# A two-layer graph attention kernel on Trainium2: edge sums by quarters of the nodes, as float32 products

## The chip, the cores and the metric

The kernel runs on one core of a Trainium2 chip. The metric is device time in microseconds (us), the median of the runs. Before the change it is 2547.23 us (three runs, 2546.41 to 2550.64). One more execution was taken with the hardware profiler; it took 2188.15 us.

## The reference

There are 3125 nodes with 768 features and 53,125 edges, which come sorted by destination; each edge has one of three types. Both layers compute the same thing, layer 1 with four heads of 192 features, layer 2 with one head of 768:

```python
xr = jnp.einsum('nd,rdf->rnf', x, W)          # a row for each node and type
oi = xr[etype, dst]; oj = xr[etype, src]
alpha = leaky_relu(oi @ q + oj @ k, 0.2)
e = exp(alpha - segment_max(alpha, dst)[dst])
a = e / (segment_sum(e, dst)[dst] + EPS)
out = segment_sum(a[:, :, None] * oj, dst) + b
```

Between the layers stands an ELU. The output is `layernorm(x + out)`. All of it is float32.

## The kernel before

The nodes are cut into 25 groups of at most 128, so that the edges of a group fill at most 17 *slots* of 128 edges each (14 for the first group); there are 422 slots in all. As edges are sorted, a group's slots hold rising node numbers. In the drawn graph a group has 104 to 128 nodes and up to 2175 edges.

The program has three stages, and every engine's order is written out by hand: each stage is a loop over steps k, one slot a step, and a table of events says at which step each function puts its instructions on the engines' queues. An engine runs its queue in that order. Pools of buffers with a fixed number of copies (`bufs`) do the rest: a buffer is filled again only when its last reader is done.

- Stage one (`phase1`, to about 690 us) multiplies x by layer 1's weights (L698), puts the rows into a table in DRAM, and computes layer 1's attention weights p for every edge and head (`pall`). `a_last` (L586) sets a flag; when it isn't zero, a second, slower kernel for any input runs afterwards (L1295 on).
- Stage two (`phase2`, about 700 to 1548 us) sums layer 1's rows and multiplies the result by layer 2's weights. `gather` (L840) has POOL fetch the 128 rows of a slot (128 x 772 float32) by an indirect DMA into one of nine buffers. `high` (L848) has ACT scale each head's 193 columns (192 features and a one) by p and round them to float32r, in H, and has DVE or POOL make the selection matrix `sel`: row is the edge, column the node, one where the edge ends at that node. `low` (L866) has DVE compute what H left out, in L. `sums` (L879) then adds sel x H and sel x L into PSUM (`acc`), two products of 386 columns each. Both parts are float32r, which goes through TensorE once. The first four odd slots are instead taken "whole" (L844): DVE puts p into the selection, and the gathered rows are multiplied in float32. `e_y` to `e_s2` turn a finished group into ELU outputs and transpose them; `d_part` (L939) multiplies them by layer 2's weights, in 18 pieces of six products, one for nearly every slot; `d_row` (L952) has ACT copy the products, and SP's queue store them to the second table.
- Stage three (`phase3`, from about 1551 us) gathers layer 2's rows into 36 buffers, computes the attention weights of a group from one column of these rows (`a_spread` to `a_put`), and sums. Here 17 of each 25 slots are whole (L1126): ACT makes the selection with p by two activations (L1141, L1142), and TensorE multiplies it by the rows in float32. The others are split in two parts as in layer 1. `e_y` to `e_out` add x and the bias, normalise and store.

The lines that matter most for TensorE in the two sums are these:

```python
T.matmul(acc[:, c, :HW], sel, a[:, c * HW:(c + 1) * HW], ...)            # L894, for H and for L
T.matmul(acc[:, h // 2, c], sel[:, h], gs[k % NG][:, h * CW:(h + 1) * CW], ...)   # L888, whole
T.matmul(acc[:, c, :HW], sel, a[:, c * HW:(c + 1) * HW], ...)            # L1168, both kinds
```

Of the kernel before, what the change touches and what calls it, by code (L numbers as in the profile page):

```python
# [8 lines left out]
F32 = mybir.dt.float32  # L9
# [11 lines left out]
P = 128  # L21
# [16 lines left out]
SL = 17  # L38
# [7 lines left out]
WHOLE = (17, 25)  # L46
# [3 lines left out]
def kernel(  # L50
# [402 lines left out]
    ends = {base(b) + slots(b) - 1 for b in range(NB)}  # L453
# [65 lines left out]
    def phase1(pre, work, psum, wH, wL, qq):  # L519
# [66 lines left out]
        def a_last():  # L586

            V.tensor_scalar(oidx, n_all[:, NB - 1:NB], col, None, op0=ALU.add)
            V.tensor_scalar(starts[0:1, 2, :NB], n_all[0:1, :NB], float(N - P), None, op0=ALU.min)
            more = work.tile([1, 2], F32, name="more", bufs=1)  # L590
            V.tensor_single_scalar(more[:, 0:1], n_all[0:1, NB:NB + 1], float(N), op=ALU.is_lt)
            V.tensor_single_scalar(more[:, 1:2], n_all[0:1, NB - 2:NB - 1], float(N - P), op=ALU.is_gt)
            V.tensor_add(bad, bad, more)
            V.tensor_add(flag, bad[:, 0:1], bad[:, 1:2])
# [230 lines left out]
    def phase2(work, psum, wH, wL):  # L825
# [3 lines left out]
        gs = share  # L829
# [8 lines left out]
        ends2 = ends  # L838

        def gather(k):  # L840
            b, j = slot(k)
            gather_rows(gs[k % NG], tab1, b, j)

        def whole(k):  # L844

            return k < 8 and k % 2 == 1

        def high(k):  # L848
            b, j = slot(k)
            g = gs[k % NG]  # L850
            if whole(k):
                sel = work.tile([P, H1, P], F32, name="L", bufs=3)
                for h in range(H1):
                    V.tensor_scalar(sel[:, h], row, dl[:, b, j:j + 1], pall[:, b, j, h:h + 1],
                                    op0=ALU.is_equal, op1=ALU.mult)
                st[k] = sel
                return
            H = work.tile([P, RW], F32R, name="H", bufs=4)
            for h in range(H1):
                c = slice(h * CW, (h + 1) * CW)  # L860
                S.activation(H[:, c], g[:, c], AF.Copy, scale=pall[:, b, j, h:h + 1])  # L861
            sel = work.tile([P, P], F32R, name="sel", bufs=4)
            (V if k % 3 == 0 else G).tensor_scalar(sel, row, dl[:, b, j:j + 1], None, op0=ALU.is_equal)  # L863
            st[k] = [sel, H]

        def low(k):  # L866
            if whole(k):
                return
            b, j = slot(k)
            g = gs[k % NG]  # L870
            H = st[k][1]
            L = work.tile([P, RW], F32R, name="L", bufs=3)
            for h in range(H1):
                c = slice(h * CW, (h + 1) * CW)
                V.scalar_tensor_tensor(L[:, c], g[:, c], pall[:, b, j, h:h + 1], H[:, c].bitcast(F32),  # L875
                                       op0=ALU.mult, op1=ALU.subtract)
            st[k].append(L)

        def sums(k):  # L879
            b, j = slot(k)  # L880
            if j == 0:
                blk[b] = {"acc": psum.tile([P, 2, 512], F32, name="acc", bufs=2)}
            acc = blk[b]["acc"]
            if whole(k):
                sel = st.pop(k)
                for h in range(H1):
                    c = slice(h % 2 * CW, (h % 2 + 1) * CW)
                    T.matmul(acc[:, h // 2, c], sel[:, h], gs[k % NG][:, h * CW:(h + 1) * CW], start=False,  # L888
                             stop=(k in ends2), skip_group_check=True)
                return  # L890
            sel, H, L = st.pop(k)
            for i, a in enumerate((H, L)):
                for c in range(2):
                    T.matmul(acc[:, c, :HW], sel, a[:, c * HW:(c + 1) * HW], start=(j == 0 and i == 0),  # L894
                             stop=(k in ends2 and i == 1), skip_group_check=True)
# [77 lines left out]
        LAG = 8  # L973
# [16 lines left out]
        for k in range(max(ev) + 1):  # L990
# [9 lines left out]
            if 0 <= k - LAG + 2 < NK:  # L1000
                low(k - LAG + 2)
            if 0 <= k - LAG + 3 < NK:
                high(k - LAG + 3)
# [11 lines left out]
    def phase3(work, psum):  # L1015
# [3 lines left out]
        NG = 36  # L1019
# [106 lines left out]
        def whole(k):  # L1126

            return k % 3 == 0 if late(k) else k * WHOLE[0] % WHOLE[1] < WHOLE[0]

        def late(k):  # L1130

            return k >= NK - SL

        def high(k):
            b, j = slot(k)
            g = gs[:, k % NG, :]
            p = blk[b]["p"][:, j:j + 1]
            if whole(k):
                sel = work.tile([P, P], F32, name="selp", bufs=4)

                S.activation(sel, row, AF.Abs, bias=dl[:, b, j:j + 1], scale=-1.0)  # L1141
                S.activation(sel, sel, AF.Relu, bias=p, scale=blk[b]["np"][:, j:j + 1])  # L1142
                st[k] = [sel, g]
                return
            H = work.tile([P, RW], F32R, name="H", bufs=4)
            S.activation(H, g, AF.Copy, scale=p)  # L1146
            sel = work.tile([P, P], F32R, name="sel", bufs=4)
            (G if late(k) else V).tensor_scalar(sel, row, dl[:, b, j:j + 1], None, op0=ALU.is_equal)
            st[k] = [sel, H]

        def low(k):
            if whole(k):
                return
            b, j = slot(k)
            g = gs[:, k % NG, :]
            L = work.tile([P, RW], F32R, name="L", bufs=3)
            V.scalar_tensor_tensor(L, g, blk[b]["p"][:, j:j + 1], st[k][1].bitcast(F32), op0=ALU.mult, op1=ALU.subtract)  # L1157
            st[k].append(L)

        def sums(k):  # L1160
            b, j = slot(k)
            sel, *parts = st.pop(k)
            if j == 0:
                blk[b]["acc"] = psum.tile([P, 2, 512], F32, name="acc", bufs=2)
            acc = blk[b]["acc"]
            for i, a in enumerate(parts):
                for c in range(2):
                    T.matmul(acc[:, c, :HW], sel, a[:, c * HW:(c + 1) * HW], start=(j == 0 and i == 0),  # L1168
                             stop=(k in ends and i == len(parts) - 1))
# [54 lines left out]
        LAG = SL + 11  # L1224
        for b in range(NB):
# [7 lines left out]
            for d, f in ((2, a_alpha), (3, a_turn), (4, a_scan), (5, a_exp), (6, a_back), (7, a_put)):  # L1233
                when(e + d, f, b)
            if b + len(xbs) < NB:
                when(e + LAG + 20, x_load3, b + len(xbs))
            for d, f in ((1, e_y), (2, e_n), (5, e_sd), (6, e_low), (8, e_out)):
                when(e + LAG + d, f, b)
        for k in range(max(ev) + 1):
            if k < NK:  # L1240
                gather(k)
            if 0 <= k - LAG < NK:
                sums(k - LAG)
            for f, a in ev.get(k, []):
                f(*a)
            if 0 <= k - LAG + 2 < NK:
                low(k - LAG + 2)
            if 0 <= k - LAG + 3 < NK:
                high(k - LAG + 3)
# [580 lines left out]
```

## Time and profile before

| | before |
|---|---|
| median of the runs | 2547.23 us |
| profiled execution, its own time | 2188.15 us |
| its span, first to last instruction | 2186.4 us |
| busy: PE, PEld, DVE, ACT, POOL | 2015.1, 1730.7, 1458.8, 1356.5, 1674.3 us |
| granted TensorE clock, mean | 0.969 |
| moved by DMA | 506.04 MB, 231 GB/s |

PE is TensorE's products, PEld its weight loads, which run beside them; DVE is VectorE, ACT ScalarE, POOL GpSimd. A record of a product lasts from its start to its modelled end, and the next one starts before that end, so distances between starts are what a stream costs. In the timeline's rows the columns are the start, the length of the merged piece, the engine, the line, the operation, what it writes and reads, the shapes and the number of records; in brackets stands idle time before the piece and what ended it. A row of waits says who waited for whom, the total, the number of times and the longest.

### The profile page before, as it was taken

How to read it: one execution, taken by the hardware profiler on the slowest of the kernel's cores; microseconds unless marked ns; L12 is line 12 of the kernel's file. 1: busy time of each engine (PE TensorE's matmuls, PEld its weight loads, DVE VectorE, ACT ScalarE, POOL GpSimd, SP SyncE). 2: the span in 40 equal slices, each digit the busy share in tenths (PEclk: the TensorE clock that was granted, in tenths of full speed). 3: DMA queues.
4: the chain of work that ended last, by engine and by line, in shares of the span. 5: the costliest groups of instructions: out<-in, count | busy, mean ns of one | idle time of the engine just before them, and what ended most of it. 6: DMA issues, size and time to landing. Idle time of an engine off the chain costs nothing.

```text
span 2186.4 us, 37632 instructions
## 1 busy us (share of the span) xinstructions
PE 2015.1 (92%) x10953; PEld 1730.7 (79%) x10953; DVE 1458.8 (67%) x4031; ACT 1356.5 (62%) x3159; POOL 1674.3 (77%) x1615
## 2 busy tenths in 40 slices
PE   5979999999987799999999999999499999989997
PEld 5979998899887799999999999999355555555555
DVE  6535554454534899999999999998155555556555
ACT  5412111122111788888888888887268887878786
POOL 4257777777777888888888888886477777777774
PEclk9989999999998899999999999999799999999999
DMA  6555545545457977888787878786789998988883
GB/s 177 188 137 173 192 145 169 174 158 183 160 168 224 311 233 246 240 246 241 237 249 226 249 231 248 231 243 191 256 303 305 315 322 309 302 295 281 294 300 108
DMA packets 156842, 506.04 MB, mean 231 GB/s; under 512 B 43875, under 2 KB 57069, under 8 KB 156628
## 3 DMA queue, kind: packets, MB, share of 16 engines
q0 software_dynamic: 81904, 331.52, 49.9%
q1 hardware_dynamic: 64494, 156.04, 20.6%
q10 hardware_dynamic: 10230, 15.98, 2.2%
q8 instruction: 91, 1.49, 0.3%
q14 instruction: 123, 1.01, 0.2%
HBM read 412.55 MB, written 95.69 MB: 232 GB/s over the span
## 4 chain that ended last, share of the span: by engine, by line
PE 61%; POOL 12%; DMA 11%; issue 11%; DVE 3%; ACT 1%; POOLq 0%; SPq 0%; DVEq 0%; ACTq 0%
PE po L949 19%; PE acc L1168 14%; PE acc L894 12%; PE po L698 8%; POOL kt L461 8%; DMA G<-ftab,ridx 6%; POOL G L461 2%; DMA kt<-kt,ridx 1%; POOL share L461 1%; PE bank L282 1%; DVE L L875 1%; PE pt L260 1%; POOL sel L863 1%; PE pt L924 1%; PE po L396 1%
## 5 line engine op out<-in xcount | busy, mean ns | idle before, releaser
L861 ACT ACTIVATE H<-share,pall 128x193 fp32r<-128x193 f32 x1672 | 618.2, 447 | 104.7 <-PE acc L894 53.5
L875 DVE SCALAR_TENSOR_TENSOR L<-share,pall,H 128x193 fp32r<-128x193 f32 x1672 | 619.0, 435 | 28.2 <-issue 19.8
L949 PE MATMUL po<-wH,hT 128*128 128x386 f32 (+1 forms) x1800 | 529.1, 339 | 0.0
L461 POOL DMA_INDIRECT G<-ftab,ridx x374 | 416.0, 1112 | 113.9 <-issue 56.1
L461 POOL DMA_INDIRECT share<-ftab,ridx x374 | 437.0, 1168 | 80.4 <-DVE L L875 34.7
L461 POOL DMA_INDIRECT kt<-kt,ridx x374 | 396.3, 1060 | 114.0 <-issue 108.5
L698 PE MATMUL po<-wH,xT 128*128 128x384 f32 x1584 | 440.3, 348 | 8.8 <-ACT share L713 4.4
L1168 PE MATMUL acc<-G,selp 128*128 128x386 f32 x1124 | 417.1, 505 | 0.0
L949 PEld LDWEIGHTS po<-wH,hT 128*128 128x128 f32 x1800 | 334.1, 189 | 0.6 <-DVE hT L937 0.5
L698 PEld LDWEIGHTS po<-wH,xT 128*128 128x128 f32 x1584 | 294.6, 191 | 13.8 <-ACT share L713 6.2
L949 PE MATMUL po<-wL,hT 128*128 128x386 f32 (+1 forms) x900 | 304.8, 339 | 0.0
L1168 PEld LDWEIGHTS acc<-G,selp 128*128 128x128 f32 x1124 | 206.0, 193 | 118.7 <-issue 16.3
L698 PE MATMUL po<-wL,xT 128*128 128x384 f32 x792 | 270.3, 341 | 0.0
L894 PE MATMUL acc<-H,sel 128*128 128x386 f32 x836 | 227.0, 353 | 19.2 <-POOL sel L863 17.6
L713 ACT COPY share<-po 128x384 f32<-128x384 f32 x144 | 67.9, 478 | 275.0 <-PE po L698 268.9
L863 POOL TENSOR_SCALAR sel<-frow,fdl 128x128 fp32r<-128x128 f32 x278 | 219.0, 788 | 12.4 <-PE acc L894 1.7
L894 PE MATMUL acc<-L,sel 128*128 128x386 f32 x836 | 217.8, 342 | 0.0
L1157 DVE SCALAR_TENSOR_TENSOR L<-G,p,H 128x772 fp32r<-128x772 f32 x141 | 143.1, 1017 | 56.1 <-ACT H L1146 56.0
L894 PEld LDWEIGHTS acc<-H,sel 128*128 128x128 f32 x836 | 148.0, 190 | 36.0 <-POOL sel L863 33.7
L949 PEld LDWEIGHTS po<-wL,hT 128*128 128x128 f32 x900 | 169.6, 188 | 0.0
L894 PEld LDWEIGHTS acc<-L,sel 128*128 128x128 f32 x836 | 155.1, 191 | 0.2 <-DVE L L875 0.2
L698 PEld LDWEIGHTS po<-wL,xT 128*128 128x128 f32 x792 | 151.8, 192 | 0.0
(246 smaller groups left out, 2688.1 us busy)
## 6 DMA issues: line engine op xcount, KB each, us to landing
ftab<-share SPq DMA_DIRECT2D x75, 386.0 KB
ftab<-r SPq DMA_DIRECT2D x75, 386.0 KB
share<-in_L_gnn_W_dram SPq DMA_DIRECT2D x36, 384.0 KB
w_d<-w2hl SPq DMA_DIRECT2D x18, 768.0 KB
sT<-dr_d SPq DMA_DIRECT2D x25, 544.0 KB
share<-in_x_dram SPq DMA_DIRECT2D x25, 384.0 KB
xb_d<-share SPq DMA_DIRECT2D x25, 384.0 KB
xr<-in_x_dram SPq DMA_DIRECT2D x23, 384.0 KB
```

The costliest lines, as they stand in the source:

```text
L260: T.transpose(pt[:, f, c * P:(c + 1) * P], a[:, (2 * i + f) * P:(2 * i + f + 1) * P], ident)
L282: T.matmul(to, a[:, 2 * i + f, :], t[:, f, :w], start=(n == 0), stop=(n == 2 * DT - 1))
L461: return G.indirect_dma_start(out=to, out_offset=None, in_=tab, in_offset=_index(i[:, j:j + 1]), bounds_check=NP * R - 1, oob_is_err=False)
L698: m = T.matmul(po[:, :HALF], xT[:, s, t, :], w[:, i, sl], start=(n == 0), stop=(n == 3 * DT - 1))
L713: S.copy(to, po[:, :HALF].rearrange("p (h f) -> p h f", h=2))
L861: S.activation(H[:, c], g[:, c], AF.Copy, scale=pall[:, b, j, h:h + 1])
L863: (V if k % 3 == 0 else G).tensor_scalar(sel, row, dl[:, b, j:j + 1], None, op0=ALU.is_equal)
L875: V.scalar_tensor_tensor(L[:, c], g[:, c], pall[:, b, j, h:h + 1], H[:, c].bitcast(F32), op0=ALU.mult, op1=ALU.subtract)
L894: T.matmul(acc[:, c, :HW], sel, a[:, c * HW:(c + 1) * HW], start=(j == 0 and i == 0), stop=(k in ends2 and i == 1), skip_group_check=True)
L949: T.matmul(po[:, :wd], hT[:, k, t, :], w[:, r * DT + t, sl], start=(t == 0 and n == 0), stop=(t == DT - 1 and n == 2))
L1157: V.scalar_tensor_tensor(L, g, blk[b]["p"][:, j:j + 1], st[k][1].bitcast(F32), op0=ALU.mult, op1=ALU.subtract)
L1168: T.matmul(acc[:, c, :HW], sel, a[:, c * HW:(c + 1) * HW], start=(j == 0 and i == 0), stop=(k in ends and i == len(parts) - 1))
```

## The change

The 128 nodes of a group are cut into four quarters of 32. A slot's edges end in one or two neighbouring quarters, listed in `WINDOW` for each of the 17 slots. Both layers' sums become float32 products of the gathered rows with a selection of 32 columns that holds p, one product for each quarter of the slot, written to that quarter's 32 partitions of PSUM (and so on that quarter of TensorE's columns). The slots of a group are taken in seven rounds (`ROUNDS`) of two or three, whose quarters mostly differ, and a round's products are put on the queue together, one quarter after the other.

In stage two, `high` is four DVE operations on at most 64 columns, `low` and the copies to H go away, the rows are gathered in the rounds' order (`in_turn`), there are 14 row buffers for nine, and sums follow a gather by 6 steps, not 8. In stage three, `high` is two ACT operations on at most 64 columns (DVE's one for odd slots of the last group), all rounds of a group follow two steps apart once its weights p are there, and there are 44 row buffers for 36. A new test, at the start of stage three, counts the edges that lie outside their slot's quarters and adds the count to the flag, which is therefore set there and not in `a_last`.

```diff
+WINDOW = ((0,), (0,), (0,), (0, 1), (0, 1), (0, 1), (1,), (1, 2), (1, 2), (1, 2), (2,), (2, 3), (2, 3), (2, 3),
+          (2, 3), (3,), (3,))
+
+ROUNDS = ((0, 7, 15), (1, 8, 16), (2, 9), (3, 11), (4, 12), (6, 14, 10), (5, 13))
...
+    def rounds(b):
+        return [[j for j in r if j < slots(b)] for r in ROUNDS]
...
-        gs = share
+        gs = share + [work.tile([P, RW], F32, name=f"g{i}", bufs=1) for i in range(5)]
...
+        def in_turn(k):
+
+            b, i = slot(k)
+            return b, [j for r in rounds(b) for j in r][i]
 
         def gather(k):
-            b, j = slot(k)
-            gather_rows(gs[k % NG], tab1, b, j)
...
+            gather_rows(gs[k % NG], tab1, *in_turn(k))
 
         def high(k):
...
+            b, j = in_turn(k)
+            lo, hi = WINDOW[j][0] * 32, WINDOW[j][-1] * 32 + 32
+            sel = work.tile([P, H1, 64], F32, name="selp", bufs=6)
+            for h in range(H1):
+                V.tensor_scalar(sel[:, h, :hi - lo], row[:, lo:hi], dl[:, b, j:j + 1], pall[:, b, j, h:h + 1],
+                                op0=ALU.is_equal, op1=ALU.mult)
+            st[b, j] = sel, gs[k % NG]
...
+            o = [(i, t) for r in rounds(b) for i in r for t in WINDOW[i]]
+            for h in range(H1):
+                c = slice(h % 2 * CW, (h % 2 + 1) * CW)
+                for i, t in o:
+                    if i not in rounds(b)[n[0]]:
+                        continue
+                    u = [x for x, y in o if y == t]
+                    sel, g = st[b, i]
+                    T.matmul(acc[32 * t:32 * t + 32, h // 2, c], sel[:, h, 32 * (t - WINDOW[i][0]):][:, :32],
+                             g[:, h * CW:(h + 1) * CW], start=(i == u[0] and h % 2 == 0), stop=(i == u[-1]),
+                             skip_group_check=True)
...
-        LAG = 8
+        LAG = 6
...
-        NG = 36
+        NG = 44
...
+        def high(b, n):
+
+            for j in rounds(b)[n]:
+                p = blk[b]["p"][:, j:j + 1]
+                lo, hi = WINDOW[j][0] * 32, WINDOW[j][-1] * 32 + 32
+                sel = work.tile([P, 64], F32, name="selp", bufs=10)[:, :hi - lo]
+                if b == NB - 1 and j % 2:
+                    V.tensor_scalar(sel, row[:, lo:hi], dl[:, b, j:j + 1], p, op0=ALU.is_equal, op1=ALU.mult)
+                else:
+
+                    S.activation(sel, row[:, lo:hi], AF.Abs, bias=dl[:, b, j:j + 1], scale=-1.0)
+                    S.activation(sel, sel, AF.Relu, bias=p, scale=blk[b]["np"][:, j:j + 1])
+                st[b, j] = sel
...
+            o = [(j, t) for r in rounds(b) for j in r for t in WINDOW[j]]
+            for c in range(2):
+                for j, t in o:
+                    if j not in rounds(b)[n]:
+                        continue
+                    u = [x for x, y in o if y == t]
+                    T.matmul(acc[32 * t:32 * t + 32, c, :HW], st[b, j][:, 32 * (t - WINDOW[j][0]):][:, :32],
+                             gs[:, (base(b) + j) % NG, c * HW:(c + 1) * HW], start=(j == u[0]), stop=(j == u[-1]))
...
+            s = base(b) + LAG + max(slots(b) - SL, -1)
+            for n in range(len(ROUNDS)):
+                when(s + 2 * n - 2, high, b, n)
+                when(s + 2 * n, sums, b, n)
+            s += 2 * len(ROUNDS)
```

## The prediction

> **What bounds the kernel now.** I read the busy slices of the page first, to split the span into stages; then the same counts for two windows; then the timeline of TensorE in each, since busy shares of pipelined matmuls overlap and only start-to-start distances can be summed.
>
> ```profile
> PE   5979999999987799999999999999499999989997
> PEclk9989999999998899999999999999799999999999
> DMA  6555545545457977888787878786789998988883
> ```
>
> A slice is 54.7 us. Slices 14 to 28 are the second stage (layer 1's sums with layer 2's product), 29 to 40 the third (layer 2's sums). TensorE is full in both at a clock of 0.9 or more; DMA is at 7 to 8 tenths in the second stage and at 9 in most of the third.
>
> ```profile
> 878.30:1502.00 623.70, 614.36 (x3460) 599.64 (x3459) 589.64 (x1723) 537.29 (x1445) 545.94 (x538) 1.00 0.80 241
> 1625.20:1891.60 266.40, 255.67 (x1065) 150.67 (x1066) 151.49 (x354) 222.07 (x433) 208.82 (x190) 0.99 0.92 314
> ```
>
> The columns are the window, its length, busy time of PE, PEld, DVE, ACT, POOL, then clock, DMA share and GB/s. The first window is 19 groups of nodes (32.8 us each). Now TensorE in it, for one slot and the sixth of a product that goes with it:
>
> ```profile
> 1008.96 0.53 PE L894 MATMUL acc<-H,sel 128*128 128x386 f32 x2
> 1009.33 0.51 PE L894 MATMUL acc<-L,sel 128*128 128x386 f32 x2
> 1009.68 0.34 PE L949 MATMUL po<-wH,hT 128*128 128x386 f32 x1
> 1009.86 0.34 PE L949 MATMUL po<-wL,hT 128*128 128x386 f32 x1
> 1010.03 0.52 PE L949 MATMUL po<-wH,hT 128*128 128x386 f32 x2
> 1010.39 0.33 PE L949 MATMUL po<-wL,hT 128*128 128x386 f32 x1
> 1010.56 0.34 PE L949 MATMUL po<-wH,hT 128*128 128x386 f32 x1
> ```
>
> A slot's four split products hold TensorE from 1008.96 to 1009.68, 0.71 to 0.72 us; the six of L949 until 1010.74, 1.06 us. A group is 17 x 0.71 + 18 x 1.06 + 0.6 (six transposes) = 31.8 us of the 32.8. The last 1.0 us is mostly this:
>
> ```profile
> PEld acc L894 <- POOL sel L863: 18.9, 38, 1.5
> ```
>
> 18.9 us over 19 groups. So TensorE's own stream sets the second stage, and whatever the change saves on DVE and ACT there is worth at most that 1 us a group. The price of a float32 product stands in two rows:
>
> ```profile
> L888 PE MATMUL acc<-share,L x32: 324/327/528, 709.5 to 718.6; 128*128 128x193 f32 x32
> L1168 PE MATMUL acc<-G,selp x1124: 485/487/1013, 1583.0 to 2173.0; 128*128 128x386 f32 x188
> ```
>
> 32 records for the 16 products of four whole slots, 1124 for some 562: a float32 product is two passes on TensorE, each with its weight load.
>
> ```profile
> 715.40 1.47 PE L888 MATMUL acc<-share,L 128*128 128x193 f32 x8
> 1743.30 0.22 PE L1050 MATMUL bc<-d,one 1*128 1x128 bf16 x1
> 1743.45 0.62 PE L1168 MATMUL acc<-H,sel 128*128 128x386 f32 x2
> 1743.91 0.52 PE L1168 MATMUL acc<-L,sel 128*128 128x386 f32 x2
> 1744.27 1.46 PE L1168 MATMUL acc<-G,selp 128*128 128x386 f32 x4
> 1745.66 0.23 PE L1117 MATMUL pa<-fident,e 17*128 17x17 f32 x1
> 1745.82 1.57 PE L1168 MATMUL acc<-G,selp 128*128 128x386 f32 x4
> ```
>
> A pass over 193 columns is (1.47 - 0.327) / 7 = 0.163 us, over 386 columns (1.46 - 0.487) / 3 = 0.325 us.
>
> **Layer 1, step by step.** Removed: 418 split slots x 0.71 us and 4 whole ones x 8 x 0.163 us, 302 us of TensorE. Added: the quarters of a group's 17 slots are 27 (7 slots with one, 10 with two), of the first group's 14 slots 23; 24 x 27 + 23 = 671, times four heads 2684 products, 5368 passes of 193 columns. A product of 32 columns streams as many columns as one of 128, so without overlap this is 5368 x 0.163 = 875 us. All depends on how far products for different quarters run at once. No row here has a product in any quarter but the first, so the trace gives only the ends: 875 us with no overlap, a quarter of it, 219 us, with four at once (261 us as the rounds are made: 0,7,15 and the others keep each quarter for two passes a head, 1.31 us a round, but round 6,14,10 needs quarter 2 twice, 2.61; 10.45 us a group).
>
> Here the row comes first: two records to a product, so the queue holds, for quarters 0 to 3, passes 0,0,1,1,2,2,3,3. The Trainium skill (TensorE: Matmul & The Clock Gate, Part 3, "What overlaps and what doesn't") says that matmuls start and end strictly in program order, and that tiles in different column groups do run together, with 2.38 times the speed measured for three. By its speed alone the sum would be near 261 us. By its order, the second pass of quarter 0 waits for the first to leave quarter 0, and quarter 1 can't start ahead of it: only one product's second pass and the next one's first run together, one pass per product, 2684 x 0.163 = 438 us. The rule of order speaks against the change, and I take 438, which lies between both ends.
>
> Changing between whole-array and quarter products: the same skill (TensorEngine Tiling (Array Packing), Key Properties) says that a change of tiling drains TensorE, with no price. The trace bounds it: the four passes from 1744.27 end at 1744.27 + 4 x 0.325 = 1745.57, the next stream starts at 1745.82, and one tiny product of 17 columns lies between, with two changes if it is one: 0.25 us, and the same around L1050. So 0 to 0.125 us a change; I take 0.1. Seven rounds a group, in and out, 350 changes: 35 us (0 to 44).
>
> What lies beside: DVE loses four subtractions (436 ns) and gains four selections of at most 64 columns where the 128-column form of L854 took 338; ACT loses four copies (447 ns). Both have more room than before, and POOL loses 278 selections of 0.79 us. All that is hidden, apart from the wait for POOL: 1.0 us a group becomes 0.5 for late rows (-12 us). The gathers stay on POOL's queue, one for one, in another order; nothing is put ahead of them. A round now waits for the last of its slots, and the product's sixth queued behind it on TensorE waits too, with ACT's copy of that product; 14 buffers in place of 9 and a longer group are the cover, and without it each late row costs its lateness (26.1 us in all for the 35 that ACT waits for now). Sum for stage two: 438 + 35 - 302 - 12 = +159 us.
>
> **Layer 2.** From 1620 to 2100 the rows list 339 gathers in 480 us: 1.42 us a slot, 24.1 us a group. TensorE's stream of it: 11.5 whole slots x 1.30, 5.5 split ones x 0.73, 2.6 for spreading, transposes and scores: 21.6 us. DMA at about 0.9 busy would need 21.7. After: 54 products a group. One pass each: 54 x 0.325 + 14 changes x 0.1 + 2.6 = 21.6 us, the same. ACT's two activations on 64 columns in place of 128 (0.88 us) are hidden, as DVE's. 44 row buffers in place of 36 let DMA run further ahead: I take -10 us for the stage, with -45 (DMA never idle) to +30 (each group waits for its last row, then 17.6 us of products) as bounds. The new test of the windows is 34 small fills and six operations on 425 columns, some 6 us of DVE by its fills (55 ns) and L1077-like rows (0.32 us for 153 columns), while the first rows are still being gathered (1552 to 1590): nothing; uncovered 6 us. SP's queue keeps its order; the last stores are issued as before.
>
> Profiled execution: 2188.15 + 159 - 10 = 2337 us. The median of the runs is 2547.23, 359 us over the profiled execution, and no view says where those lie. Taken as a factor (1.164) I get 2720, as a constant 2696; I forecast **2705 us**, with 2640 to 2790 as its own range (changes at 0 or 0.125 us, layer 2's bounds, factor or constant).
>
> **The rivals.** Four quarters at once: if each quarter queues its own passes, stage two is 261 + 35 - 302 - 12 = -18 us. Layer 2's TensorE falls to 10.4 + 1.4 + 2.6 = 14.4 us a group, DMA sets it at about 22.4: -40 us. 2130 profiled, about **2485 us**, faster. For it: different partitions of PSUM, different operands. It decides as soon as a group's products in layer 1 take less than 12 us. Its gain is small even so, as layer 1's split products were already one pass each.
>
> No overlap, or weight loads that wait for the running product: 875 + 35 - 302 - 12 = +596, and layer 2 at 35.1 + 4.0 = 39.1 us a group, +370: 3154 profiled, about **3590 us**. Against it: in the trace weight loads lie under products everywhere (PEld 600 of 624 us beside PE 614), and the skill's measured speed.
>
> That it doesn't do what it says: an edge outside its slot's quarters would set the flag and run the whole fallback. In the drawn dst, sorted and grouped as the kernel does it, none of 53,125 edges lies outside, so I give it 1 in 100.
>
> **How the numbers follow.** One pass per product 0.52, four at once 0.37, no overlap 0.10, fallback 0.01. Differences below 0.2%, 5 us, can't be told from none. Of four at once, 0.31 is faster, 0.03 the same and 0.03 slower (late rows or dear changes eat 60 us); the one-pass case is slower but for 0.01 the same. Faster 0.31, same 0.04, slower 0.65. The range 2430 to 2800 takes in the first two cases and leaves no overlap and the tails out.
>
> **What would show it.** Quarter products starting one pass (0.163 us) apart for each two records, TensorE still full in stage two, and groups of 39 us there: right. Groups of 32 us with eight records in two passes' time: the first rival. DVE and ACT under half busy in either. If stage two's idle time before the quarter products is over 1 us a group, for rows or for DVE, the cover I counted on is gone. The forecast falls if the passes of one product don't hold up the next, or if changes cost far more than 0.125 us.

## The result and the profile after

| | before | after |
|---|---|---|
| median of the runs | 2546.82 us (2544.31 to 2550.64) | 2632.01 us (2624.0 to 2634.09) |
| ratio, with its 95% interval | | 1.0327 (1.0301 to 1.0353) |
| profiled execution, its own time | 2188.15 us | 2634.09 us |
| its span | 2186.4 us | 2632.3 us |
| busy: PE, PEld, DVE, ACT, POOL | 2015.1, 1730.7, 1458.8, 1356.5, 1674.3 us | 2135.9, 1508.2, 1046.8, 700.2, 1329.6 us |
| granted TensorE clock, mean | 0.969 | 0.859 |

The change made the kernel 85 us slower. The forecast said slower, with 2705 us, and its range holds 2632. But the two columns of the profile can't be subtracted: the 359 us between the profiled execution of before and the median of its runs, which the prediction carried along unexplained, go with the chip. The same kernel before, run beside the experiments below, took 2497.36 us on one chip and 2179.78, 2180.41 and 2188.16 us on three others. I call chips of the first sort *long-time chips* (the measured medians of this result come from there too) and the others *short-time chips* (the profile that the prediction read belongs there by its time). Each chip served once, so a lasting trait of a chip and its condition at that hour can't be told apart. A repeat of before on the long-time chip gave the profile to compare with, and a repeat of the change on a short-time chip the other half. The lengths of the stages, each from the first to the last start of its products in the timeline (stage one from about 40 us on), and the spans:

| | stage one | layer 1's sums to the last piece of layer 2's product | layer 2's sums | span |
|---|---|---|---|---|
| before, short-time chip | 653 | 840 | 591 | 2186.4 |
| change, short-time chip (`e9_change_again`) | 656 | 829 | 551 | 2137.3 |
| before, long-time chip (`e1_before_again`) | 932 | 830 | 636 | 2503.3 |
| change, long-time chip (the result) | 969 | 841 | 722 | 2632.3 |

The result's chip took 49 us more for before than e1's did, so the 37 us between the last two rows of stage one, which the change hardly touches, are put down to the chip. Between the two short-time profiles the change gains 49 us (42 between the medians taken on one such chip, 2179.78 and 2138.11), 40 of them in layer 2's stage (the forecast's first rival gave -40 for it), and between the long-time ones layer 2's stage is 86 *longer*. Stage two, where the forecast put +159 us, moved by 11 us in either direction. That is no more than its old form differs from run to run: it took 825 us in `e8_layer2_quarters_6_later` and 842 in `e3_layer2_quarters`, which both keep it. So single profiles can't tell a change of stage two from none.

These are the busy slices of the page after; a slice is 65.8 us, slices 16 to 28 are stage two, 29 to 40 layer 2's sums:

```profile
PE   6868777778777775999999999999557777777776
PEclk9977777888878877999999999999777788777888
DMA  6443333333333256777777777775778777777772
```

Before had a 9 nearly throughout in the first two rows of the third stage, and 8 or 9 in the last. Now TensorE is at 7 of 10 there, its clock at 7 or 8, and DMA at 7: nothing is full. Stage two looks as before. The first stage, which the change hardly touches, is also at a clock of 7 to 8 in this execution; it is in the long-time chip's profile of before as well. The same by windows, first the profile after (stage two, then layer 2's sums), then before on a long-time chip and the change on a short-time chip, each in layer 2's sums. The columns are those of the windows above: length, busy PE, PEld, DVE, ACT, POOL, clock, DMA share, GB/s.

```profile
1023.00:1864.00 841.00, 822.63 (x8214) 673.32 (x8215) 514.08 (x2115) 112.74 (x199) 417.21 (x415) 0.99 0.77 240
1897.00:2620.00 723.00, 535.25 (x3291) 158.08 (x3287) 168.34 (x495) 416.49 (x1061) 402.09 (x402) 0.80 0.73 239
```

```profile
1854.00:2491.00 637.00, 577.74 (x2290) 338.49 (x2289) 330.16 (x759) 485.51 (x932) 444.70 (x408) 0.95 0.82 268
```

```profile
1574.00:2125.00 551.00, 444.16 (x3286) 150.10 (x3286) 166.91 (x494) 413.33 (x1060) 407.89 (x401) 0.89 0.90 313
```

In the last row DMA has taken the place of TensorE as the limit: 0.90 busy at 313 GB/s, beside TensorE's 444 of 551 us. On the long-time chip the same instructions take 171 us longer, with a DMA share of 0.73.

Now the step on which the forecast rested. TensorE's timeline after, in the middle of stage two:

```profile
1422.56 0.35 PE L878 MATMUL acc<-share,selp 128*32 128x193 f32 x1
1422.57 0.36 PE L878 MATMUL acc<-g,selp 128*32 128x193 f32 x3
1422.75 0.33 PE L878 MATMUL acc<-share,selp 128*32 128x193 f32 x1
1422.76 0.34 PE L878 MATMUL acc<-g,selp 128*32 128x193 f32 x3
```

Four records start together, and the next four 0.18 to 0.19 us later: all four quarters run at once, both passes of each product with the other products' passes. That is the first rival's picture (eight records in two passes' time), not the forecast's (two records each 0.163 us).

### The profile page after: what moved, and what is told of

Same layout as the page of the kernel before. It is cut to its first block, busy times and chain, and to the rows that moved or that the text cites. A ratio compares the mean times of both kernels' runs of the same rounds, so it can differ in the third digit from the quotient of the medians.

```text
span 2632.3 us, 43673 instructions
## 1 busy us (share of the span) xinstructions
PE 2135.9 (81%) x15615; PEld 1508.2 (57%) x15615; DVE 1046.8 (40%) x3669; ACT 700.2 (27%) x1612; POOL 1329.6 (51%) x1326
## 4 chain that ended last, share of the span: by engine, by line
PE 61%; issue 10%; another core or an unknown queue 4%; DVE 3%; ACT 2%; DMA 1%; POOL 0%; POOLq 0%; ACTq 0%; DVEq 0%; SPq 0%
PE po L934 19%; PE acc L1134 15%; PE acc L878 11%; PE po L702 11%; PE bc L1033 1%; DVE F L1087 1%; DVE sT L1043 1%; PE pt L909 1%; DVE B L1089 1%; PE px L679 1%; PE pq L1054 0%; PE pa L1081 0%; DMA kt<-kt,ridx 0%; ACT sT L1039 0%
## 5 line engine op out<-in xcount | busy, mean ns | idle before, releaser
L1134 PE MATMUL acc<-G,selp 128*32 128x386 f32 x2684 | 471.6, 617 | 143.0 <-issue 133.7
L857 DVE TENSOR_SCALAR selp<-frow,fdl,pall 128x64 f32<-128x64 f32 (+1 forms) x1688 | 391.2, 335 | 53.4 <-PE acc L878 44.8
L1134 PEld LDWEIGHTS acc<-G,selp 128*32 128x32 f32 x2684 | 127.8, 127 | 399.4 <-issue 334.6
L466 POOL DMA_INDIRECT share<-ftab,ridx x239 | 240.5, 1006 | 216.8 <-PE acc L878 168.4
L942 ACT COPY r<-po 128x386 f32<-128x386 f32 (+1 forms) x150 | 72.2, 482 | 653.1 <-PE po L934 458.5
L878 PE MATMUL acc<-share,selp 128*32 128x193 f32 x3472 | 226.7, 334 | 6.9 <-issue 5.9
L466 POOL DMA_INDIRECT g<-ftab,ridx x135 | 136.0, 1007 | 122.8 <-PE acc L878 95.0
L1120 ACT ACTIVATE selp<-selp,p,np 128x64 f32<-128x64 f32 (+1 forms) x414 | 177.5, 429 | 70.5 <-DVE np L1107 56.5
L878 PEld LDWEIGHTS acc<-share,selp 128*32 128x32 f32 x3472 | 134.6, 111 | 69.0 <-issue 34.9
L878 PE MATMUL acc<-g,selp 128*32 128x193 f32 x1896 | 136.8, 330 | 1.5 <-issue 1.5
```

Source lines behind the costliest of these rows:

```text
L466: return G.indirect_dma_start(out=to, out_offset=None, in_=tab, in_offset=_index(i[:, j:j + 1]), bounds_check=NP * R - 1, oob_is_err=False)
L857: V.tensor_scalar(sel[:, h, :hi - lo], row[:, lo:hi], dl[:, b, j:j + 1], pall[:, b, j, h:h + 1], op0=ALU.is_equal, op1=ALU.mult)
L878: T.matmul(acc[32 * t:32 * t + 32, h // 2, c], sel[:, h, 32 * (t - WINDOW[i][0]):][:, :32], g[:, h * CW:(h + 1) * CW], start=(i == u[0] an ...
L942: S.copy(o[:, c * HW:c * HW + wd], po[:, :wd])
L1134: T.matmul(acc[32 * t:32 * t + 32, c, :HW], st[b, j][:, 32 * (t - WINDOW[j][0]):][:, :32], gs[:, (base(b) + j) % NG, c * HW:(c + 1) * HW], ...
```

## Experiments

Two questions were open. First, which of the two mechanisms holds in the sums. Second, why layer 2's stage gets longer, although its products are cheap. For the second, theory A was: TensorE idles while a group's weights p are worked out, since the rounds of the group before are queued too early, and its clock falls; then putting the rounds later, or giving TensorE filler in the gap, should recover time. The rival: TensorE itself issues slowly there, whatever stands ahead of it in the queue.

### Repeating before, and each layer's part alone

`e1_before_again` is the kernel before with nothing changed. `e2_layer1_quarters` has the change in stage two alone, `e3_layer2_quarters` in stage three alone (each with its half of the diff shown above, e3 with the test of the windows). A few lines of each:

```diff
# e2: stage two of the change, stage three of before
+        gs = share + [work.tile([P, RW], F32, name=f"g{i}", bufs=1) for i in range(5)]
+            gather_rows(gs[k % NG], tab1, *in_turn(k))
# e3: stage two of before, stage three of the change
-        NG = 36
+        NG = 44
+        def high(b, n):
```

> The kernel before, unchanged, with a profile. Theory A (the 359 us between the profiled execution and the median lie in stage one and are not the change's): this time the profile agrees with the median, near 2547 us, and stage one lasts about 1010 us as in the profile of the changed kernel, with stages two and three at their first profile's 839 and 635 us give or take 40. Rival B (the whole program runs slower outside that one profile): all three stages are longer by the same 16%, stage two near 975 us.

> Layer 1's sums by quarters, layer 2's as before. Theory A (quarters run together, so stage two costs the same; the loss is stage three's): within 1% of before, 2530 to 2570 us. Rival B (the loss comes with every added instruction): about 50 of the 85 us, 2597 us, as layer 1 has twice layer 2's products.

> Layer 2's sums by quarters, with the test of the windows, layer 1's as before. Theory A: the whole loss, about 2630 us, in stage three. Rival B: about 35 us of loss, 2582 us.

Measured, on one long-time chip, against before: e1 2501.56 us, 0.9998 (0.9972 to 1.0023); e2 2515.08 us, 1.0058 (1.0035 to 1.0081); e3 2570.40 us, 1.025 (1.0172 to 1.0328). This time profile and median agree, and the time over the short-time profile lies mostly in stage one, as theory A of e1 said. e2 is within 1%, as its theory A said; e3 loses 73 us, most of the 85 but not all. The product of the last two ratios, 1.031, is the whole change's 1.0327 within the intervals. So most of the loss is in layer 2's half of the change: the third stage is 707 us in e3, against 636 in e1 and 635 in e2. Layer 1's quarters cost some 14 us there; stage two is 840 us in e2 and 830 in e1.

e1's trace also shows what is different on a long-time chip. TensorE in stage one:

```profile
880.49 0.33 PE L698 MATMUL po<-wL,xT 128*128 128x384 f32 x1 [0.91 <-issue]
...
883.30 0.48 PE L698 MATMUL po<-wH,xT 128*128 128x384 f32 x1 [1.66 <-issue]
884.03 0.68 PE L698 MATMUL po<-wL,xT 128*128 128x384 f32 x1 [0.25 <-issue]
...
886.12 0.48 PE L698 MATMUL po<-wH,xT 128*128 128x384 f32 x1 [0.92 <-issue]
```

The starts here are 0.70 us apart or a multiple of it, where the same products follow each other after 0.175 us in the rest of the stage. Where a step seems to be missing, a weight load has it: those of 885.43, 887.55 and 888.95 each start 0.70 us after the product before them. "issue" means that nothing the profile knows was waited for. Such a stretch lasts mostly 12 to 15 us in this stage and comes once in nearly every group (879 to 893, 913 to 927, 948 to 962 us). TensorE's own waits in stage one sum it up, in e1:

```profile
PE po L698 <- issue: 128.4, 174, 3.6
```

On the short-time chip, TensorE's waits of before in stage one have no row that ends with issue at all.

Does the low clock make the steps, or the reverse? The windows of e1 around this stretch (columns as above) give the order in time:

```profile
878.60:882.00 3.40, 1.57 (x6) 0.81 (x5) 0.00 (x0) 0.00 (x0) 2.48 (x4) 1.00 0.81 290
882.00:893.20 11.20, 4.71 (x9) 2.32 (x9) 2.11 (x5) 0.00 (x0) 6.79 (x7) 0.51 0.23 62
893.20:895.70 2.50, 2.46 (x8) 2.48 (x9) 0.00 (x0) 0.96 (x2) 0.00 (x0) 0.50 0.49 37
```

The steps begin at full clock, some 3 us before it falls to half, and when they are over, eight products follow each other at half clock, 0.32 us apart. So in this stretch the low clock comes after the slow issue, and by itself it makes a product 0.32 us, not 0.70.

Nor is it TensorE alone. SyncE issues the loads of a group's data. Here are two of them (T and sT) for one group, in e1 and then in before on the short-time chip:

```profile
877.17 0.00 SPq L490 DMA_DIRECT2D T<-ed_d  x1
889.68 0.35 SPq L496 DMA_DIRECT2D sT<-dr_d  x1
```

```profile
639.28 0.83 SPq L490 DMA_DIRECT2D T<-ed_d  x1
642.01 0.35 SPq L496 DMA_DIRECT2D sT<-dr_d  x1
```

From one to the other are 12.5 us in e1 and 2.7 us in before. Some of it may be a wait; but between the two, e1's trace has SyncE's register and semaphore instructions 0.70 us apart as well (879.76, 880.46, 881.17), where they are under 0.1 us apart in before. Over the 25 groups the median of this distance is 7.7 or 7.8 us in all five profiles of long-time chips and 3.2 us in all nine of short-time ones.

### How far the quarters run ahead: `e4_quarter_by_quarter`

The change with layer 1's products of a round put in another order: all of quarter 0's first, then quarter 1's.

```diff
-            for h in range(H1):
-                c = slice(h % 2 * CW, (h % 2 + 1) * CW)
-                for i, t in o:
-                    if i not in rounds(b)[n[0]]:
-                        continue
+            for q in range(4):
+                for h in range(H1):
+                    c = slice(h % 2 * CW, (h % 2 + 1) * CW)
+                    for i, t in o:
+                        if t != q or i not in rounds(b)[n[0]]:
+                            continue
```

> The changed kernel, but in layer 1 a round's products are queued all of quarter 0 first (four heads, eight passes), then all of quarter 1, and so on. If each quarter takes any number of its own passes off the common queue: 1.5 us for a round's 32 passes as before, 2632 us. If a quarter takes only a pass or two ahead of the one that runs: the quarters follow each other nearly one at a time, 4 to 5 us for such a round, 150 rounds of them, about 400 us more.

Measured: 2889.78 us, 1.1549 (1.1478 to 1.1619); stage two is 1148 us, between the two cases of the expectation. The timeline shows a round of three quarters and one of four:

```profile
1401.08 2.87 PE L879 MATMUL acc<-share,selp 128*32 128x193 f32 x24
...
1406.20 3.56 PE L879 MATMUL acc<-share,selp 128*32 128x193 f32 x32
```

The change's own round of 32 passes takes 1.52 us, eight steps of 0.163 and the 0.33 of a record (7 x 0.163 + 0.33 = 1.47). Here it is (3.56 - 0.33) / 0.163 = 19.8 steps from the first start to the last. If each quarter starts d steps after the one before it, the last start is at 3d + 7, so d = 4.3; the round of three gives (2.87 - 0.33) / 0.163 = 15.6 = 2d + 7, d = 4.3 again. The trace of the second round shows it directly: four records alone, then pairs, so the next quarter's first pass starts with the fifth pass of the one before. A quarter with eight passes in a row thus holds the next one back until some four of its passes are left. With the two passes of one product in a row it holds nothing back. So order does matter, but at a depth of about four passes, not of one.

### Later rounds and filler: `e5_rounds_3_later`, `e6_rounds_6_later`, `e7_fill_the_gap`, `e10_rounds_3_later_again`

```diff
# e5, e10: LAG + 3;  e6: LAG + 6
-        LAG = SL + 10
+        LAG = SL + 13
# e7
+        def fill(b):
+            po = psum.tile([P, 512], F32, name="pq", bufs=1)
+            for i in range(24):
+                T.matmul(po[:, :256], junk[:, :P], junk, start=True, stop=True)
...
+            when(s - 1, fill, b)
```

> The changed kernel with layer 2's rounds three steps later (17 + 13 steps after a group's first gather, not 17 + 10), so that more products of the old group stand on TensorE's queue between the transposes of the new group's scores and its first round. Theory A (the loss is TensorE idle while the new group's softmax runs, and the half clock that follows): about half of the idle 4 us a group is covered, stage three falls from 722 to about 640 us, the whole from 1.033 to about 1.00 of before. Rival B (TensorE's instruction supply: as many instructions, so the same slow stretch in each group): no change beyond 1%.

> The same with six steps (17 + 16). Theory A: the softmax of the new group is wholly covered by products of the old one, the clock stays up, DMA sets stage three: about 580 to 600 us, the whole near 0.97 of before. Rival B: no change beyond 1%. If row buffers (44) run short, the gathers wait and stage three is longer than with three steps.

> The changed kernel with 24 bfloat16 products of 256 columns (2.6 us at full clock) before each group's first round in layer 2; nothing reads them. Theory A in its part about the clock (an idle TensorE gets half clock for the first rounds): the first two rounds take about 3 us in place of 6.4, and the filler costs what it hides: 1.02 to 1.035 of before. If the idle time alone is the loss and the clock is not: some 50 us slower than the change. Rival B (instruction supply): slower, by the share of the 48 added instructions in a group's 270, about 30 us.

These three ran on a short-time chip: 2138.80 us, 0.9804 (0.9777 to 0.9832); 2140.04 us, 0.9814 (0.979 to 0.9839); 2152.94 us, 0.9871 (0.9846 to 0.9897). Against a kernel before of 2180.41 us all are faster, by 1.3 to 2.0%. Only theory A of e6 had named a gain, and for another reason: no theory knew that the sign depends on the chip. So the change itself had to be run on such a chip too, beside one of them:

> The changed kernel itself, once more. Some executions of the kernel before take about 2180 us and stage one 690 us, others about 2500 us and 971 us, and it goes by the chip. Theory A (the loss has a part that every chip shows, TensorE idle during a group's softmax, and a part that belongs to chips on which TensorE has slow stretches): where before takes about 2180 us, the change is within 1% of before, 2160 to 2200 us; where before takes about 2500 us, 1.033 of it again. Rival C (the loss is the change's own everywhere): 1.03 on either kind.

> Layer 2's rounds three steps later, once more, beside the change. Theory A: 1 to 2% faster than the change where before takes 2180 us; where before takes about 2500 us, the slow stretches stay and it is 0.99 to 1.01 of before. Rival C: as far from the change as it was from before, 2% on either kind.

e9, the change as it is: 2138.11 us, 0.9795 (0.9753 to 0.9837). e10: 2138.27 us, 0.9809 (0.9773 to 0.9846). Neither theory of e9 (within 1% of before, 1.03) nor of e10 (2% beside the change, in either direction) was met: rounds three or six steps later are worth nothing. The filler costs some 14 us (2152.94 on its chip, 2138.8 for e5 beside it), although it did raise the clock for the products behind it. First filler and first two rounds of a group in e7, then the same rounds in e9:

```profile
1668.69 5.28 PE L1103 MATMUL pq<-frow 128*128 128x256 bf16 x24 [2.70 <-DVE oh L1060]
1673.90 3.11 PE L1141 MATMUL acc<-G,selp 128*32 128x386 f32 x32
```

```profile
1845.40 6.08 PE L1134 MATMUL acc<-G,selp 128*32 128x386 f32 x32 [1.63 <-ACT selp L1120]
```

The two rounds take half as long, the 3 us that its theory A had said for them, but the filler itself takes 5.28 us, and part of the gap stays: the filler writes the PSUM buffer of the scores and so waits until DVE has read them. On short-time chips neither the idle time nor the clock that theory A named is what sets this stage. On a long-time chip it wasn't tried: all these runs were on short-time ones.

What e9 does show is what this stage looks like when nothing disturbs it. The page's slices (53.4 us each; slices 30 to 40 are layer 2's sums) and the waits in them:

```profile
PE   5979999999989599999999999999858788788786
PEclk9979999999999799999999999999968989889898
DMA  6555554455548887777777777776489999999993
```

```profile
DVE a L1071 <- DMA G<-ftab,ridx: 227.8, 27, 12.1
```

DMA is at 9, and DVE's first operation on a group's scores waits 227.8 us in all for rows: the gathers set the pace, as the rival said. Their issues follow each other after 1.32 us a slot in the middle of the stage, 1.42 in before; a group is 22.5 us, beside the 22.4 that the rival gave DMA. What lets the gathers run faster, cheaper products or the 44 row buffers that came with them for 36, no run separates.

### Layer 2's part alone on such a chip: `e8_layer2_quarters_6_later`

```diff
# stage two of before, stage three of the change with
-        LAG = SL + 10
+        LAG = SL + 16
```

> Layer 1 as before, layer 2 by quarters with its rounds six steps later. Theory A: stage three as in the run with six steps, stage two as before: 0.965 to 0.975 of before. Rival B: as layer 2's quarters alone, 1.025.

Measured: 2141.14 us, 0.9833 (0.9801 to 0.9865), beside e6's 0.9814 with both layers. Neither theory's number was met (0.965 to 0.975, 1.025). Layer 2's stage in its new form gives the whole gain; layer 1's quarters give nothing that these runs can tell: stage two is 825 us in e8, in its old form, and 825 in e6 beside it, by quarters.

### Two heads at a time, and the small products: `e11_two_heads_no_burst_3`, `e12_no_burst_1`

In e1 each slow stretch of stage one begins some 4 to 6 us after a run of 17 tiny score products (at 874.73 and 909.18 for the stretches from 879 and 913). Two kernels replace these by one or two wide ones on other data, and so leave these scores out: e11 in layer 2, e12 in stage one. e11 also orders layer 1's products by quarters again, but for two heads at a time, so that four passes of a quarter stand in a row, not eight.

```diff
# e11, layer 1
-            for h in range(H1):
+            for q in range(8):
+                for h in (q // 4 * 2, q // 4 * 2 + 1):
...
+                        if t != q % 4 or i not in rounds(b)[n[0]]:
# e11, layer 2
-            for j in range(SL):
-                T.matmul(pq[:, j * nq:(j + 1) * nq], s["sT"][:, j * P:(j + 1) * P], ...)
+            T.matmul(pq[:, :SL * nq], s["sT"][:, :P], s["sT"][:, :SL * nq], start=True, stop=True)
# e12, stage one
-            for j in range(SL):
-                T.matmul(pq[:, j // hs, (j % hs) * nq:(j % hs + 1) * nq], s["sT"][:, j * P:(j + 1) * P], ...)
+            for c in range(2):
+                n = min(hs, SL - c * hs) * nq
+                T.matmul(pq[:, c, :n], s["sT"][:, :P], s["sT"][:, :n], start=True, stop=True)
```

> The changed kernel with two edits in separate stages. In layer 1 a round's products are queued quarter by quarter for two heads at a time, so four passes of one quarter stand in a row. If a quarter takes about four passes ahead (from the run with eight in a row, 3.56 us for a round of 32 passes): a round lasts about 2.2 us or less and stage two is at most 100 us longer than the change's 829 us; if it takes only one or two ahead: near 2.9 us and 200 us. In layer 2 the 17 small products of a group that give the query scores are replaced by one of 153 columns on other data; the query scores of layer 2 are left out. Theory H (on chips where stage one takes 970 us, TensorE runs one instruction in 0.70 us for some 13 us after each such burst): there, layer 2's slow stretches go and stage three falls from 722 to below 640 us; on a chip where stage one takes 690 us, stage three stays within 15 us of 551. Rival D (the stretches come with a group or with a count of instructions): 722 us stays where stage one takes 970.

> The changed kernel with the 17 small products of a group in stage one (layer 1's query scores) replaced by two wide ones on other data; the query scores of layer 1 are left out. Theory H: on a chip where before's stage one takes 970 us, this one's takes about 700 us, while stage three stays at 722; on the other kind of chip nothing changes by more than 10 us. Rival D: stage one stays at 970 us on such a chip.

Both ran on a short-time chip: e11 2142.24 us, 0.98 (0.9768 to 0.9831); e12 2133.98 us, 0.9759 (0.9727 to 0.979). There are no slow stretches there, and the stages altered last as long as e9's (layer 2's sums 552 us in e11 beside 551, stage one 652 in e12 beside 656), so these two can't say whether the tiny products trigger them. e1's own layer 2 can, in part: it has 25 such runs of 17, and none is followed by a stretch. One of them:

```profile
2295.22 0.58 PE L1071 MATMUL pq<-q2s,sT 128*128 128x9 bf16 x17
2295.66 2.84 PE L1168 MATMUL acc<-G,selp 128*128 128x386 f32 x8
2298.04 0.81 PE L1168 MATMUL acc<-H,sel 128*128 128x386 f32 x2
2298.69 0.51 PE L1168 MATMUL acc<-L,sel 128*128 128x386 f32 x2
2299.04 2.76 PE L1168 MATMUL acc<-G,selp 128*128 128x386 f32 x8
```

The eight passes of 2295.66 and of 2299.04 are 0.33 us apart, as on the short-time chip. So tiny products alone don't make a stretch, even on such a chip. Of the depth, e11 does tell:

```profile
1104.19 1.54 PE L879 MATMUL acc<-g,selp 128*32 128x193 f32 x24
```

Four passes of a quarter in a row cost next to nothing: 1.54 us for the 24 passes of three quarters, where eight in a row took 2.87; eight steps without any loss are 1.47. Stage two is 833 us, e9's 829: better than either case of the expectation.

## Where the loss on the long-time chip lies

In the result's trace, one round of layer 2 in the middle of the stage:

```profile
2243.12 0.88 PE L1134 MATMUL acc<-G,selp 128*32 128x386 f32 x6
2245.64 0.69 PE L1134 MATMUL acc<-G,selp 128*32 128x386 f32 x1 [1.64 <-issue]
2247.09 1.56 PE L1134 MATMUL acc<-G,selp 128*32 128x386 f32 x2 [0.76 <-issue]
2249.93 0.87 PE L1134 MATMUL acc<-G,selp 128*32 128x386 f32 x2 [1.28 <-issue]
2251.35 0.80 PE L1134 MATMUL acc<-G,selp 128*32 128x386 f32 x1 [0.55 <-issue]
```

And the same round of a group in e9:

```profile
1851.72 1.50 PE L1134 MATMUL acc<-G,selp 128*32 128x386 f32 x12
```

Twelve records take 1.50 us in e9 and nearly 9 us here (2243.12 to the next round's small product at 2252.08), with steps of some 0.70 us or a multiple: the picture of stage one. TensorE's own waits of the whole stage after:

```profile
PE acc L1134 <- issue: 133.7, 127, 2.3
```

e3 has the same row with 108.0 us (142 times), before on the long-time chip 1.2 us (3 times) for its sums, and before and the change on short-time chips have none. That is idle time of TensorE, and while the records between these gaps also run slowly, the 133.7 us alone are most of the 171 us by which the stage is longer than e9's. A lower clock comes with it, 0.80 beside 0.89 there; in the round shown, the first late steps (from 2243.5 on) again lie in a window of full clock (1.00 from 2242.4 to 2245.8), and half clock follows.

Before is spared. On the long-time chip the products of its third stage show no such steps (the lines from 2295.22 above; e2, which keeps that stage, shows none either), while stage one of the same execution has them. Its 45 us over the short-time chip are something else: its gathers follow each other after 1.50 us, not 1.42, for a reason that I did not find. With the change (the result, e3 and e4) nearly every group of layer 2 has a stretch of some 5 to 9 us, which begins about 10 us after its small products. So the loss is the meeting of the two, such a chip and the new stage three. What in the new stage brings the stretches on, the quarter products, their coming in rounds or the 44 buffers, is not shown. The density of instructions alone isn't it: stage two has the densest of all, four products and their loads in each 0.163 us, and only its first group shows a stretch (1028 to 1045 us), which is about what it loses there (841 against 829 us).

## Why the prediction was right or wrong, point by point

- **Direction and size: right by luck, from a cause that it did not name.** 2705 us was forecast for stage two slower by 159 us and layer 2 nearly unchanged (-10). Stage two hardly moved, and layer 2 did, by 86 us, on the sort of chip that the result came from. On the other sort the forecast's sign is wrong. That the time lies in the range is owed to this exchange.
- **The failed step: "the second pass of quarter 0 waits for the first to leave quarter 0, and quarter 1 can't start ahead of it".** The first half is true (in e4 the passes of one quarter stand 0.163 us apart), the second isn't. I took the Trainium skill's strict order of starts and ends (TensorE: Matmul & The Clock Gate, Part 3, "What overlaps and what doesn't") down to single passes. The runs show passes of four quarters together (0.163 us for four records), hardly a loss with four passes of a quarter in a row (e11), and d = 4.3 steps per quarter with eight (e4), where starts in strict order would need 7 or more. Here the page and e4 differ, and the measurement decides: the order does not hold between quarters. The sum that rested on it, 438 us, becomes the rival's 261: eight steps to a round of 32 passes. Layer 2's "one pass each" falls with it.
- **Change of tiling: mis-sized.** I took 0.1 us for each, at most 0.125. Around the round at 1402:

```profile
1402.13 0.34 PE L934 MATMUL po<-wH,hT 128*128 128x384 f32 x1
1402.40 1.52 PE L878 MATMUL acc<-g,selp 128*32 128x193 f32 x32
1403.85 0.44 PE L934 MATMUL po<-wH,hT 128*128 128x386 f32 x1
1404.13 0.33 PE L934 MATMUL po<-wL,hT 128*128 128x386 f32 x1
```

  The round starts 0.27 us after the last product, where 0.176 would be the product's own; its eight steps would end at 1403.70 and the next product starts at 1403.85; the one after follows 0.28 us later, where 0.176 is usual. That is 0.09 + 0.15 + 0.10 = 0.34 us for in and out, 0.17 a change, and 350 changes are 60 us, not 35. It is one round, read closely, but the next point bears it out. The skill's "drain" at a change of tiling (TensorEngine Tiling (Array Packing), Key Properties) fits it; the price is this trace's.
- **Cover of stage two: right.** A group is now 10.45 + 7 x 0.34 + 18 x 1.06 + 0.6 = 32.5 us by its parts, and 32.56 from one group's transposes to the next's in e9: no idle time is left, so the 1.0 us a group that waited for POOL's selections is gone altogether (-25 us, I took -12). Sum: 261 + 60 - 302 - 25 = -6 us. It can't be told from none: a group of the old form is 32.2 us on average in e8, 32.8 in the profile before, as its waits for POOL differ, and the new one 32.5 wherever it ran. What cheap rounds brought, changes of tiling took: layer 1's split products were already one pass each, as the rival's last sentence had it.
- **DVE's selections: hidden as said, but not under half busy.** The page after has

```profile
L857 DVE TENSOR_SCALAR selp<-frow,fdl,pall 128x64 f32<-128x64 f32 (+1 forms) x1688 | 391.2, 335 | 53.4 <-PE acc L878 44.8
```

  335 ns on at most 64 columns, where the 128-column form took 338: narrowing saves nothing. In stage two DVE is busy 514 of 841 us (window above), over the half that the forecast had given as a sign; still it waits for TensorE (44.8 us), not the other way round.
- **Layer 2: the rival's sum holds on short-time chips, neither sum on long-time ones.** The rival said -40 us and 2130 us profiled; measured are 591 to 551 us and 2139.18. On long-time chips mine was -10, within -45 to +30; measured is +86, or +71 in e3 alone. The term that was missing, at nothing in every sum, is TensorE's time without a wait, 133.7 us in the result.
- **The 359 us: left unexplained, and decisive.** Between the two profiles of before, on the two sorts of chip, 317 us of span lie: 279 in stage one (932 against 653), 45 in layer 2's sums, -10 in stage two. That is neither a factor nor a constant over all stages. I applied both and added the change to either. The stages that such a chip stretches have to be known before a change to them can be priced there; no view of the profile that I had showed them.

What stays open: why TensorE issues one instruction per 0.70 us in those stretches. I looked for instruction fetches: the queue for them moved 91 packets and 1.49 MB before, 128 and 2.10 MB after, 16 KB a packet; but their landings did not line up with the ends of the stretches, nor with their starts: in e1's stage one the last fetch before a stretch begins 1 to 36 us ahead of it, at a distance that drifts from group to group, and a fetch takes about 1.06 us in e1 and before alike. What sets a stretch off, why SyncE is slow with TensorE, which part of the change brings the stretches into layer 2, whether later rounds or filler would help where they occur, and what differs between the chips were not settled.

## What to carry to other kernels

On short-time chips the stage gained in which whole-array float32 products (two passes) were the most, with more row buffers beside them, and the stage of split products of one pass did not. Price each change of tiling at 0.17 us, as measured here, and put many products between two of them. Put no more than about four passes of one quarter in a row. And when the profiled execution and the median of the runs differ by 16%, the profile stands for another regime: ask which stage carries the difference before adding a change's saving to either number.

## What the runs showed of the hardware that was not expected

- One kernel, before, took 2180 us on some chips and 2497 to 2547 us on others, with stage one at 653 or 932 us and stage two at 840 or 830 in the two profiles. The sign of the change follows: 0.9795 (0.9753 to 0.9837) on one, 1.0327 (1.0301 to 1.0353) on the other.
- On such chips TensorE issued single instructions, products or weight loads, about 0.70 us apart for 12 to 15 us at a time in stage one, with no wait that the profile shows, next to stretches of the same code at 0.175 us. SyncE's instructions were 0.70 us apart in the same stretch, and the granted clock fell some 3 us after it began.
- Four column quarters ran float32 products fully at once: eight passes in the time of two. With eight passes of one quarter in a row the next quarter started 4.3 passes later; with four in a row nothing was lost that shows.
